# A decoder's first self attention: another order of the score units, maxima moved by DMA, results gathered by DMA

## The chip, the cores and the metric

The kernel runs on one core of one Trainium2 chip. The metric is the time of one execution on the device, in microseconds; several runs are timed and their median is given. A separate execution is profiled. In the profile, PE is the matrix engine, PEld its weight loads, DVE the vector engine, ACT the scalar engine, POOL the general engine, and SP an engine that here only issues DMAs. L191 means line 191 of the kernel before.

## What is computed

Two decoder layers in a row on x, a tensor of 4 x 1024 x 256 floats. Only the first step is changed, a causal self attention with 16 heads of 16, its output projection, the addition of x and a layer norm:

```python
q, k, v = jnp.split(x @ w_in.T + b_in, 3, axis=-1)      # to 16 heads of 16
scores = jnp.einsum('bhqd,bhkd->bhqk', q * 0.25, k)
scores = scores + causal_bias                           # 0 below the diagonal, -inf above
attn = jax.nn.softmax(scores, axis=-1)
out = jnp.einsum('bhqk,bhkd->bhqd', attn, v)
x = _layernorm(x + (out.reshape(4, 1024, 256) @ w_out.T + b_out))
```

The later steps (cross attention, feed forward, and the second layer) are the same in both kernels.

## The kernel before, in words

The function self_attention (L186) handles 16 groups of four heads: group s belongs to batch s//4. The heads' queries and keys lie spread over the 128 partitions, head g of the group in partitions 32g to 32g+15 (tiles qp and kp). A score matmul therefore contracts over a strip of 32 rows of PE, and a unit works on two heads: pair 0 means the strips of heads 0 and 1, pair 1 those of heads 2 and 3.

Scores are computed twice. An **a unit** (L312) computes scores with queries on the output partitions, and DVE takes maxima over keys from PSUM (L332, L348). There are 18 of them per group, nine of each pair. For the diagonal blocks (units 7 and 8) a matmul of the identity with a mask is added after the scores (L346, recorded at L191). When a group's maxima are complete, L356 joins and negates them; L366 turns them with eight transposes, and L370 adds them to the queries, into row 16 of each strip of a second tile, qs. The keys hold a one in that row, so a **b unit** (L380), which computes the scores again with keys on the output partitions, yields scores less the maximum. ACT takes their exponential (L399), POOL clears what is above the diagonal (L402), and weighted (L420, recorded at L191, output acc) multiplies with the values. A value tile has 17 columns per head, the last of which is one, so that the sum of the exponentials comes out as a 17th row. ACT copies acc to SBUF (L439), L451 transposes it, DVE divides (L454, L455), L467 transposes back, and out_projected (L472) applies the output weights and adds to x.

The order of the work is written out by hand. at(when, f, ...) records an event, and all events run in order of when; PE instructions, DMAs and some others keep that order on their engine. A slot of T = 20 steps belongs to one group's a units: place j (0 to 17) of slot s stands at 20s+1+j and issues, together and round by round, one a unit of group s and one b unit of the group before, two places behind (L542 to L551). What stands between two places, in the gap, runs on the full array: the projections of later queries and keys (L275, four matmuls of 512 columns as two events per slot), values (L258), transposes, and the weighted sums (L420), which are split into pieces so that some gaps take 384 columns and others 128 (L525 to L538). Seven PSUM banks rotate among scores, projections and transposes (pool ps_l0a), and one holds acc. Queries and keys are spread over the strips by DMAs on SP's queue (L293), four per tile, of 64 KB each.

The units' strips come from these lines:

```python
rows = [slice(64 * pair + 32 * g, 64 * pair + 32 * g + 32) for g in range(2)]
...
units.append((a_unit, s, (7, 8, 0, 1, 2, 3, 4, 5, 6)[j // 2], 1 - j % 2))
sb, jb = divmod(18 * (s - 1) + j - 2, 18)
if 0 <= sb < 4 * NB:
    units.append((b_unit, sb, jb // 2, jb % 2))
```

Of the kernel before, what the change touches and what calls it, by code (L numbers as in the profile page):

```python
# [16 lines left out]
P = 128  # L17
# [12 lines left out]
def decoder_kernel(ctx: ExitStack, tc: tile.TileContext, a: dict, out: bass.AP):  # L30
# [155 lines left out]
    def self_attention(wk, pss, psa):  # L186
# [29 lines left out]
        vts, nmps, nmts = [], [], []  # L216
        for i in range(2):
            vt = wk.tile([P, NC, 17 * H + 16], F32, tag=f"v{i}", name=f"v{i}", bufs=1)
            nc.gpsimd.memset(vt, 1.0)
            vts.append(vt)  # L220
            nmp = wk.tile([P, 4, NC, 3], F32, tag=f"nmp{i}", name=f"nmp{i}", bufs=1)
            nc.gpsimd.memset(nmp, -3.0e38)
            nmps.append(nmp)
            nmt = wk.tile([P, NC, 4, 32], F32, tag=f"nmt{i}", name=f"nmt{i}", bufs=1)
            nc.gpsimd.memset(nmt, 0.0)
            nmts.append(nmt)

        bo2 = wk.tile([P, E], F32, tag="bo2", name="bo2", bufs=1)
        t = bank()
        for e in range(2):  # L230
            mm(t[:, :E], l0a_bv[:, e : e + 1].to_broadcast([P, P]), l0a_wo[:, e, :], e == 0, e == 1)
        nc.vector.tensor_tensor(bo2, t[:, :E], l0a_bo, ALU.add)
# [6 lines left out]
        xTs, ons, sts, qss, pts, accs, ots = {}, {}, {}, {}, {}, {}, {}  # L239
# [18 lines left out]
        def values(b, i):  # L258
            t = bank()
            for j in range(2):  # L260
                c = 2 * i + j
                for e in range(2):
                    mm(
                        t[:, j * E : (j + 1) * E],
                        xTs[b][:, e, c * P : (c + 1) * P],
                        l0a_w[:, e, 2 * E :],
                        e == 0,
                        e == 1,
                    )
            (nc.vector.tensor_copy, nc.scalar.copy)[i % 2](  # L270
                vts[b % 2][:, 2 * i : 2 * i + 2, : 17 * H].rearrange("p c (h r) -> p c h r", r=17)[:, :, :, 0:16],
                t.rearrange("p (c h d) -> p c h d", c=2, h=H),
            )

        def projected(kind, i, q):  # L275
            w0, bias, scale = {"k": (E, l0a_bk, 1.0), "q": (0, bq4, 0.25)}[kind]
            b, h = divmod(i, 2)
            if q == 0:
                sts[kind, i] = wk.tile([P, S], F32, tag="s" + kind, name="s" + kind, bufs=1)
            t = bank()  # L280
            for e in range(2):
                mm(
                    t,
                    l0a_w[:, e, w0 + h * P : w0 + (h + 1) * P],
                    xTs[b][:, e, q * 512 : (q + 1) * 512],
                    e == 0,
                    e == 1,
                )
            nc.scalar.activation(
                sts[kind, i][:, q * 512 : (q + 1) * 512], t, AF.Identity, bias=bias[:, h : h + 1], scale=scale  # L290
            )

        def spread(kind, s):  # L293
            pads = {"k": kpads, "q": qpads}[kind]
            pad = pads[s % len(pads)]
            st = sts[kind, s // 2]
            for g in range(4):
                r = 64 * (s % 2) + 16 * g
                pe(nc.sync.dma_start(out=pad[32 * g : 32 * g + 16, :], in_=st[r : r + 16, :]))
# [12 lines left out]
        def a_unit(s, u, pair):  # L312

            t = [bank() for _ in range(2)]
# [20 lines left out]
            else:  # L335
                q0 = 4 * (u - 7)
                for j in range(4):
                    cols = slice((q0 + j) * P, (q0 + j + 1) * P)
                    rounds.append([
                        (t[g][:, j * P : (j + 1) * P], qt[rows[g], cols], kt[rows[g], cols], j == 0, False)  # L340
# [3 lines left out]
                def after():  # L344
                    for g in range(2):
                        mm(t[g], ident_bf, cmask4.rearrange("p j n -> p (j n)"), False, True)  # L346
# [8 lines left out]
        def highest(s):  # L355
            nc.vector.tensor_reduce(  # L356
                nmts[s % 2][:, :, :, 16], nmps[s % 2].rearrange("p g q i -> p q g i"), AX.X, ALU.max, negate=True
            )

        def shifted_queries(s):  # L360
            nmt = nmts[s % 2]
            qs = qss[s] = wk.tile([P, S], F32, tag="qs", name="qs")
            for q in range(2):
                t = bank()
                for j in range(4):
                    pe(nc.tensor.transpose(  # L366
                        t[:, j * P : (j + 1) * P], nmt[:, 4 * q + j, :, :].rearrange("p g r -> p (g r)"), ident
                    ))
                cols = slice(q * 512, (q + 1) * 512)
                nc.vector.tensor_tensor(qs[:, cols], t, qpads[s % 2][:, cols], ALU.add)  # L370
# [49 lines left out]
        def weighted(s, qh, i, pieces, first=False, last=False):  # L420
# [6 lines left out]
            for kc, c0, q0, n in pieces:  # L427
                for g in range(4):
                    mm(
                        acc[32 * g : 32 * g + 32, q0 : q0 + n],  # L430
                        vts[b % 2][:, kc, 17 * (4 * t4 + g) : 17 * (4 * t4 + g) + 32],
# [4 lines left out]
            if last:  # L436
                if qh == 0:
                    ots[s] = wk.tile([P, S], F32, tag="ot", name="ot")
                nc.scalar.copy(ots[s][:, qh * 512 : (qh + 1) * 512], acc)  # L439

        def normalised(s, i):
            b, t4 = divmod(s, 4)
            if t4 == 0 and i == 0:
                ons[b] = wk.tile([P, NC, E], F32, tag="on", name="on", bufs=1)
            ot = ots[s]
            c0 = 4 * i
            on = ons[b][:, :, t4 * 64 : (t4 + 1) * 64].rearrange("p c (g d) -> p c g d", g=4)
            t = bank()
            for j in range(4):
                c = c0 + j  # L450
                pe(nc.tensor.transpose(t[:, j * P : (j + 1) * P], ot[:, c * P : (c + 1) * P], ident))  # L451
            v = t.rearrange("p (c g r) -> p c g r", c=4, g=4)
            rs = small.tile([P, 4, 4], F32, tag="rs8", name="rs8", bufs=2)
            nc.vector.reciprocal(rs, v[:, :, :, 16])  # L454
            nc.vector.tensor_tensor(  # L455
                on[:, c0 : c0 + 4],
                v[:, :, :, 0:16],
                rs.unsqueeze(3).to_broadcast([P, 4, 4, 16]),
                ALU.mult,
            )  # L460

        def turned_back(b, e, q):
            if (e, q) == (0, 0):
                ots[b, "n"] = wk.tile([P, 2, S], F32, tag="onT", name="onT", bufs=1)
            t = bank()
            for j in range(4):
                pe(nc.tensor.transpose(  # L467
                    t[:, j * P : (j + 1) * P], ons[b][:, 4 * q + j, e * P : (e + 1) * P], ident
                ))
            nc.scalar.copy(ots[b, "n"][:, e, q * 512 : (q + 1) * 512], t)  # L470

        def out_projected(b, c):  # L472
            onT = ots[b, "n"]
            t = bank()[:, :E]
            for e in range(2):
                mm(t, onT[:, e, c * P : (c + 1) * P], l0a_wo[:, e, :], e == 0, e == 1)
            y = wk.tile([P, E], F32, tag="y0", name="y0")
# [10 lines left out]

        T = 20
        for b in range(NB):  # L490
            t0 = 4 * b * T
            for i in range(4):
                q, e = divmod(i, 2)
                if b:
                    at(t0 - 2 * T + (3.5, 7.5, 9.5, 11.5)[i], x_transposed, b, e, q)
                else:
                    at(-60 + i + q, x_transposed, b, e, q)
                at(t0 + (i // 2 - 1) * T + (3.5, 7.5)[i % 2], values, b, i)
                at(t0 + 5 * T + 3.5 + 4 * i, turned_back, b, e, q)
            for c in range(NC):  # L500
                u = (117.5, 135.5, 151.5, 155.5, 157.5, 171.5, 175.5, 177.5)[c]
                at(t0 + u if b < 3 else t0 + 6 * T + c, out_projected, b, c)
        for i in range(2 * NB):
            t0 = 2 * i * T
            for q in range(2):
                if i == 0:
                    at(-57.5 + 2 * q, projected, "k", i, q)
                    at(-57.4 + 2 * q, projected, "q", i, q)
                else:
                    at(t0 - 2 * T + ((13.5, 17.5) if i % 2 == 0 else (9.5, 13.5))[q], projected, "k", i, q)  # L510
                    at(t0 - T + (9.5, 13.5)[q], projected, "q", i, q)
            for j in range(2):
                at(t0 + (j - 1) * T + 2.6 if i else -50 + j, spread, "k", 2 * i + j)
                at(t0 - (1 - j) * T + (16.5, 2.7)[j] if i else -50 + j, spread, "q", 2 * i + j)
        for s in range(4 * NB):
            at((s + 1) * T + 0.3, highest, s)
            at((s + 1) * T + 1.4, shifted_queries, s)
            if s < 3:
                at(s * T + 0.7, later_x, s + 1)
            for i in range(2):  # L520
                at((s + 2) * T + 1.5 + 4 * i, normalised, s, i)
            t0 = (s + 1) * T

            full = {0: (3, 7, 9, 13), 1: (9, 13), 2: (13, 17), 3: (3, 7, 9, 13)}
            for i, place in ((0, 6), (4, 14), (5, 16), (7, 22)):  # L525
                qh, kc = (0, 0) if i == 0 else (1, i - 3)
                n = 512 if (place + 1) % T in full[(s + 1 + place // T) % 4] else 384
# [1132 lines left out]
```

## Time and profile before

| what | us |
|---|---|
| median of 3 runs | 2229.46 |
| lowest and highest | 2228.82, 2235.07 |
| the profiled execution's own time | 2231.37 |
| its span in the profile | 2229.6 |
| first and last maximum L356 (groups 0 and 15) | 63.95, 704.82 |
| first instruction of the next step on PE | 750.12 |
| slot 3, from L356 to L356 | 42.20 |
| PE, DVE, ACT, POOL busy in that slot | 42.20, 27.10, 22.57, 6.30 |
| DMA of 64 KB to qp or kp, from issue to landing | 2.3 |

The changed stage is the first third of the span. A busy time is the time in which at least one instruction of the engine runs; matmuls are pipelined, and the profile models their ends, so the duration of a matmul row is longer than its share. The distance between the start of one group of matmuls and the start of the next is the safer measure. A matmul on f32 is recorded as two instructions, which the text calls passes. In a row of the timeline the columns are start, duration, engine, line, operation, output and inputs, the rows and columns of the array, the shape and the number of instructions joined in the row.

### The profile page before, as it was taken

The numbers are of one execution on the slowest core, as the hardware profiler recorded it, in microseconds if no ns is written. First come the engines' busy times: TensorE is split into PE (matmuls) and PEld (weight loads), VectorE is DVE, ScalarE is ACT, GpSimd is POOL, SyncE is SP. The second block draws the span as 40 slices with busy tenths as digits, with TensorE's granted clock in tenths as the row PEclk, the third lists the DMA queues.
The fourth block names the chain that finished last, engine by engine and source line by source line (L and its number), as shares of the span: only waits on it lengthen the run. The fifth ranks groups of instructions, "written<-read, shape, count | busy, mean of one in ns | idle before, by whom it ended". The sixth has DMA issues, their size and how long they took to land.

```text
span 2229.6 us, 39020 instructions
## 1 busy us (share of the span) xinstructions
PE 2100.6 (94%) x14708; PEld 1255.9 (56%) x14708; DVE 1491.3 (67%) x3287; ACT 1119.0 (50%) x2861; POOL 510.4 (23%) x1113
## 2 busy tenths in 40 slices
PE   7999999999999899989899989989999999999996
PEld 4554554555454456556556556656666655565654
DVE  4766667776775556658997888886972465555644
ACT  1455554554555365556666655554543234545444
POOL 1111111111111265445455443000000111111102
PEclk9999999999999999999999999999999999999998
DMA  4101100000000100000000100000000010010101
GB/s 111 39 6 53 37 9 15 11 16 15 6 16 1 39 1 20 1 1 1 1 1 1 34 1 22 1 0 1 1 1 1 2 20 15 15 29 10 29 1 38
DMA packets 24445, 34.85 MB, mean 16 GB/s; under 512 B 5953, under 2 KB 19649, under 8 KB 24257
## 3 DMA queue, kind: packets, MB, share of 16 engines
q1 hardware_dynamic: 22640, 31.20, 6.1%
q8 instruction: 117, 1.92, 0.4%
q10 hardware_dynamic: 1616, 1.16, 0.2%
q14 instruction: 72, 0.58, 0.1%
HBM read 15.56 MB, written 4.19 MB: 9 GB/s over the span
## 4 chain that ended last, share of the span: by engine, by line
PE 71%; DVE 20%; ACT 6%; issue 1%; POOL 1%; DMA 1%; SPq 0%; ACTq 0%; POOLq 0%; DVEq 0%
PE s L191 21%; PE t L590 15%; PE s L1196 10%; PE s L590 8%; PE acc L191 6%; DVE gt L946 4%; PE acc L1196 3%; PE t L774 2%; ACT u L749 2%; DVE nmp L332 2%; DVE x L169 1%; DVE nmx L745 1%; DVE bnst L136 1%; DVE gt L956 1%; DVE ht L932 1%
## 5 line engine op out<-in xcount | busy, mean ns | idle before, releaser
L399 ACT ACTIVATE p<-s 128x512 f32<-128x512 f32 x576 | 312.2, 595 | 291.9 <-PE s L191 283.7
L332 DVE TENSOR_REDUCE nmp<-s 128x1 f32<-128x512 f32 (+3 forms) x640 | 298.6, 522 | 153.8 <-PE s L191 153.0
L191 PE MATMUL s<-qs,kp 32*128 32x512 f32 (+3 forms) x1536 | 347.9, 521 | 0.0
L191 PE MATMUL s<-kp,qp 32*128 32x128 f32 (+3 forms) x2304 | 327.7, 407 | 2.4 <-DMA qp<-sq 2.1
L757 POOL TENSOR_SCALAR p<-u,rs 128x128 f32<-128x128 f32 x512 | 215.9, 441 | 284.8 <-DVE rs L753 185.0
L191 PEld LDWEIGHTS s<-kp,qp 32*128 32x128 f32 x2304 | 165.5, 189 | 136.1 <-ACT p L399 46.2
L402 POOL TENSOR_SCALAR_AFFINE_SELECT p<-p 128x256 f32<-128x256 f32 x256 | 99.6, 407 | 567.8 <-ACT p L399 567.8
L749 ACT ACTIVATE u<-s,nmx 128x154 f32<-128x154 f32 x512 | 192.9, 393 | 46.7 <-DVE nmx L745 30.6
L154 POOL TENSOR_TENSOR rstd<-ve,neghalf 128x4 f32<-128x4 f32 (+1 forms) x56 | 58.6, 1046 | 573.6 <-DVE ve L152 569.2
L191 PE MATMUL acc<-p,v 128*32 128x384 f32 (+3 forms) x2016 | 167.9, 420 | 0.1
L191 PEld LDWEIGHTS s<-qs,kp 32*128 32x128 f32 x1536 | 138.8, 183 | 29.1 <-DVE nmp L332 8.4
L590 PE MATMUL t<-xT,xw 128*128 128x512 f32 x256 | 123.3, 605 | 11.8 <-DVE xT L677 8.4
L1353 DVE TENSOR_REDUCE nmt<-s 128x3 f32<-128x462 f32 (+1 forms) x192 | 99.0, 578 | 45.6 <-PE s L1196 45.6
L745 DVE TENSOR_REDUCE nmx<-s 128x4 f32<-128x616 f32 x128 | 100.9, 788 | 39.5 <-PE s L590 38.2
L590 PE MATMUL t<-v,pt 128*128 128x256 f32 x512 | 116.5, 380 | 8.2 <-DVE pt L1105 8.2
L590 PE MATMUL t<-xw,ot 128*128 128x256 f32 x512 | 119.0, 387 | 2.7 <-ACT qt L731 2.6
L946 DVE SCALAR_TENSOR_TENSOR gt<-ht,cw,gt 128x256 f32<-128x256 f32 x256 | 116.4, 500 | 6.5 <-ACT gt L942 5.3
L590 PEld LDWEIGHTS s<-kt,qt 64*128 64x128 f32 x1024 | 75.9, 186 | 72.2 <-issue 50.8
L590 PE MATMUL s<-qt,xT 128*128 128x512 f32 x256 | 115.1, 592 | 0.0
L590 PEld LDWEIGHTS t<-v,pt 128*128 128x128 f32 x512 | 95.8, 190 | 30.5 <-DVE pt L1105 9.8
L348 DVE TENSOR_REDUCE nmp<-s 128x4 f32<-128x512 f32 x128 | 82.4, 686 | 44.8 <-PE s L191 44.4
L749 ACT ACTIVATION_READ_ACCUMULATOR u<-s,nmx 128x1 f32 x512 | 106.4, 208 | 0.0
(259 smaller groups left out, 3851.0 us busy)
## 6 DMA issues: line engine op xcount, KB each, us to landing
qp<-sq SPq DMA_DIRECT2D x128, 64.0 KB, 2.3
kp<-sk SPq DMA_DIRECT2D x64, 64.0 KB, 2.3
out_dram<-x SPq DMA_DIRECT2D x8, 512.0 KB, 2.9
x<-in_x_dram SPq DMA_DIRECT2D x3, 1024.0 KB, 6.5
wf<-in_L_ffn_w_dram SPq DMA_DIRECT2D x2, 1024.0 KB, 6.0
xw<-in_L_xattn_wk_dram SPq DMA_DIRECT2D x1, 1024.0 KB, 6.5
xw<-in_L_xattn_wq_dram SPq DMA_DIRECT2D x1, 1024.0 KB, 5.0
xw<-in_L_xattn_wv_dram SPq DMA_DIRECT2D x1, 1024.0 KB, 5.0
```

What stands on the lines that cost most here:

```text
L191: pe(nc.tensor.matmul(o, l, r, start=start, stop=stop))
L332: nc.vector.tensor_reduce(nmp[:, 2 * pair + g, qc, i : i + 1], t[g][:, c0 : c0 + n], AX.X, ALU.max)
L348: nc.vector.tensor_reduce(nmp[:, 2 * pair + g, q0 : q0 + 4, 0], t[g].rearrange("p (j n) -> p j n", j=4), AX.X, ALU.max,)
L399: nc.scalar.activation(p[:, g, :], t[g], AF.Exp)
L402: nc.gpsimd.affine_select(out=v, in_=v, compare_op=ALU.is_ge, fill=0.0, base=0, pattern=[[0, 2], [1, P]], channel_multiplier=-1,)
L590: pe(nc.tensor.matmul(o, l, r, start=start, stop=stop))
L745: nc.vector.tensor_reduce(nmx.rearrange("p i g -> p g i"), t, AX.X, ALU.max, negate=True)
L749: nc.scalar.activation(u[:, 2 * i + g, :], t[:, g, i, :], AF.Exp, bias=nmx[:, i, g : g + 1], accum_out=ssum[:, i, g : g + 1],)
L757: nc.gpsimd.tensor_scalar(p[:, h * P : (h + 1) * P], u[:, h, :P], rs[:, h : h + 1], 1.0, ALU.mult, ALU.mult)
L946: nc.vector.scalar_tensor_tensor(g, ht[:, i, k : k + N], cw[:, hc, k : k + 1], g, ALU.mult, ALU.add)
L1196: pe(nc.tensor.matmul(o, l, r, start=start, stop=stop))
L1353: nc.vector.tensor_reduce(nmts[s % 2][:, 3 * u : 3 * u + n, g, 17], ts[g][:, : n * LK].rearrange("p (c k) -> p c k", k=LK), AX.X, ALU.max, ...
```

## The change

The change rewrites how the pieces of this step follow each other, and three of the paths between engines.

- **Order of the a units.** The diagonal units stand at places 1, 3, 5 and 7, and the others follow in the order 4, 5, 6, 0, 1, 2, 3, with both pairs of each (a_order). The b units stand four places behind instead of two (DELAY).
- **Mask first.** The mask matmul opens the accumulation in the gap ahead of a diagonal unit (causal_mask), which takes its two banks there.
- **Maxima.** The queries are copied to qs by one DMA (second_queries). The joined maxima, 32 columns, are turned by one transpose, copied by ACT to SBUF and written to row 16 of the strips by four DMAs (maxima_turned).
- **Results.** A head has 24 columns in the value tile, 16 values and 16 shared ones for two heads, so that a sum of exponentials comes out in 16 rows. Eight DMAs per group gather values and sums into tiles on and den, untransposed (gathered). DVE takes the reciprocal of den in pieces of 128x512, and POOL multiplies (divided). The output projection reads the product as it is.
- **Equal pieces.** Weighted sums are one event per pair of units, in the odd gaps, values and projections have pieces of 256 columns.
- The bias of the output projection is computed in a later gap, the first queries are spread by ACT's queue, and the last results are gathered in two halves, partly by ACT's queue.

```diff
-        def shifted_queries(s):
-            nmt = nmts[s % 2]
-            qs = qss[s] = wk.tile([P, S], F32, tag="qs", name="qs")
-            for q in range(2):
-                t = bank()
-                for j in range(4):
-                    pe(nc.tensor.transpose(
-                        t[:, j * P : (j + 1) * P], nmt[:, 4 * q + j, :, :].rearrange("p g r -> p (g r)"), ident
-                    ))
-                cols = slice(q * 512, (q + 1) * 512)
-                nc.vector.tensor_tensor(qs[:, cols], t, qpads[s % 2][:, cols], ALU.add)
+        def second_queries(s):
+            qs = qss[s] = wk.tile([P, S], F32, tag="qs", name="qs")
+            pe(nc.sync.dma_start(out=qs, in_=qpads[s % 2]))
+        def maxima_turned(s):
+            t = bank()[:32, :P]
+            pe(nc.tensor.transpose(t, hms[s].rearrange("p g c -> p (g c)"), ident))
+            rows = wk.tile([32, P], F32, tag="mrow", name="mrow")
+            nc.scalar.copy(rows, t)
+            for g in range(4):
+                pe(nc.sync.dma_start(
+                    out=qss[s][32 * g + 16 : 32 * g + 17, :].rearrange("p (c n) -> p c n", c=NC),
+                    in_=rows[NC * g : NC * g + NC, :],
+                ))
...
+        diagonal = {1: (7, 0), 3: (7, 1), 5: (8, 0), 7: (8, 1)}
+        others = iter([(u, pair) for u in (4, 5, 6, 0, 1, 2, 3) for pair in range(2)])
+        a_order = [diagonal[j] if j in diagonal else next(others) for j in range(18)]
+
+        def causal_mask(s, j):
+            t = masks[s, j] = [bank() for _ in range(2)]
+            for g in range(2):
+                mm(t[g], ident_bf, cmask4.rearrange("p j n -> p (j n)"), True, False)
+
+        def a_unit(s, j):
+            u, pair = a_order[j]
+            t = masks.pop((s, j)) if j in diagonal else [bank() for _ in range(2)]
...
-        def normalised(s, i):
...
-        def turned_back(b, e, q):
...
+        def gathered(s, c0=0, n=S, queue=None):
...
+            cols = slice(c0, c0 + n)
+            for g in range(4):
+                r = 64 * (t4 % 2) + 16 * g
+                up = 32 * g + 16 * (g % 2)
+                down = 32 * g + 16 * (1 - g % 2)
+                pe(nc.sync.dma_start(out=ons[b][r : r + 16, e, cols], in_=ots[s][up : up + 16, cols]))
+                pe((queue or nc.sync).dma_start(out=dens[b, e][r : r + 16, cols], in_=ots[s][down : down + 16, cols]))
+
+        def divided(b, e, q):
+            cols = slice(512 * q, 512 * q + 512)
+            den, on = dens[b, e][:, cols], ons[b][:, e, cols]
+            nc.vector.reciprocal(den, den)
+            nc.gpsimd.tensor_tensor(on, on, den, ALU.mult)
...
+        def gap(s, j):
+            return (s + j // 18) * T + 1.5 + j % 18
...
+                        at(gap(2 * i - (2 if kind == "k" else 1), 6 + 2 * q), projected, kind, i, q)
...
+            at((s + 1) * T + 0.3, highest, s)
+            at(gap(s + 1, 0) - 0.1, maxima_turned, s)
+            at(gap(s, 4.3), second_queries, s)
...
+            for i in range(9):
+                g = gap(s + 1, 2 * i + 3 + DELAY)
+                for qh, kc, c0 in b_sets[i]:
+                    if (i, qh) == (2, 1):
+                        continue
+                    n = width(qh, kc)
+                    last = (i, qh) == (2, 0) or (i, kc) == (8, 7)
+                    at(g, weighted, s, qh, i, [(kc, c0, 512 - n, n)], i in (0, 3), last)
...
+            if s < 4 * NB - 1:
+                at(gap(s + 2, 5.3), gathered, s)
+            else:
+                at(gap(s + 1, 11.2), gathered, s, 0, 512, nc.scalar)
+                at(gap(s + 2, 5.3), gathered, s, 512, 512, nc.scalar)
+            for j in diagonal:
+                at(gap(s, j - 1) + 0.3, causal_mask, s, j)
...
                 if s < 4 * NB:
-                    units.append((a_unit, s, (7, 8, 0, 1, 2, 3, 4, 5, 6)[j // 2], 1 - j % 2))
-
-                sb, jb = divmod(18 * (s - 1) + j - 2, 18)
+                    units.append((a_unit, s, j))
+
+                sb, jb = divmod(18 * (s - 1) + j - DELAY, 18)
                 if 0 <= sb < 4 * NB:
                     units.append((b_unit, sb, jb // 2, jb % 2))
```

The reciprocals of a batch (divided) stand in the gaps after places 8 and 10 of the slots 4b+3 and 4b+5; for the last batch, after place 5 of slots 15 and 17 and place 12 of slot 16 (in slot 15 the build has the two behind the reduces of place 9).

## The prediction

> **What bounds the kernel now.** I read the page's busy table first, then the chain that ended last, then the busy times of whole slots, then single places of the timeline. A slot is one pass of the loop over groups of four heads (18 places); it runs from one maximum L356 to the next.
>
> ```profile
> PE 2100.6 (94%) x14708; PEld 1255.9 (56%) x14708; DVE 1491.3 (67%) x3287; ACT 1119.0 (50%) x2861; POOL 510.4 (23%) x1113
> ...
> PE s L191 21%; PE t L590 15%; PE s L1196 10%; PE s L590 8%; PE acc L191 6%; DVE gt L946 4%; PE acc L1196 3%; PE t L774 2%; ACT u L749 2%; DVE nmp L332 2%; DVE x L169 1%; DVE nmx L745 1%; DVE bnst L136 1%; DVE gt L956 1%; DVE ht L932 1%
> ```
>
> TensorE leads, and the changed stage (L191) is the largest entry. Two slots of that stage, busy times by engine:
>
> ```profile
> 144.76:186.96 42.20, 42.20 (x414) 21.72 (x410) 27.10 (x57) 22.57 (x41) 6.30 (x17) 1.00 0.15 39
> 186.96:229.19 42.23, 42.23 (x414) 21.75 (x414) 27.11 (x56) 22.57 (x41) 6.22 (x16) 1.00 0.15 39
> ```
>
> PE is busy for all 42.2 us at a granted clock of 1.00; DVE needs 27.1 and ACT 22.6. So in this stage a microsecond of PE is a microsecond of time, and work taken from DVE is worth nothing by itself.
>
> Now one place, an a unit (scores for the maxima, kp,qp) and a b unit (scores for the exponentials, qs,kp) issued together:
>
> ```profile
> 165.29 0.70 PE L191 MATMUL s<-kp,qp 32*128 32x512 f32 x2
> ...
> 165.30 0.70 PE L191 MATMUL s<-qs,kp 32*128 32x512 f32 x2
> ...
> 165.82 0.59 PE L191 MATMUL s<-kp,qp 32*128 32x512 f32 x2
> 165.84 0.59 PE L191 MATMUL s<-qs,kp 32*128 32x512 f32 x2
> 166.36 0.30 PEld L191 LDWEIGHTS s<-xT,qkv 128*128 128x128 f32 x2 [0.76 <-DVE nmp L332]
> ```
>
> Each f32 matmul is recorded as two passes. Eight passes of 512 columns are over in 166.36-165.29 = 1.07 us. From the full-array matmuls (four passes of 512 from 166.36 to 168.27) one such pass takes about 0.43 us, so eight in a row would need 3.4: the four 32-row strips of the array work side by side, a on one pair of strips and b on the other. A b unit alone takes as long:
>
> ```profile
> 719.50 1.13 PE L191 MATMUL s<-qs,kp 32*128 32x512 f32 x4
> ...
> 720.56 1.13 PE L191 MATMUL s<-wo,onT 128*128 128x256 f32 x4
> ```
>
> That is 1.06 us, so the second unit is free **when it stands on the other two strips**. What it costs on the same strips is shown in the first slot, where a units stand alone, on alternating pairs:
>
> ```profile
> 44.23 1.99 PE L191 MATMUL s<-kp,qp 32*128 32x512 f32 x12
> 46.15 1.99 PE L191 MATMUL s<-qkv,xT 128*128 128x256 f32 x8
> 48.07 1.14 PE L191 MATMUL s<-kp,qp 32*128 32x512 f32 x8
> 49.15 1.12 PE L191 MATMUL s<-xT,qkv 128*128 128x512 f32 x2
> ```
>
> Two units on two pairs: 49.15-48.07 = 1.08. Three units, the third on the first one's pair: 46.15-44.23 = 1.92. A unit that shares strips costs 0.85 us more, two passes of 0.43.
>
> **Part 1: which strips the units take.** Before, L549 gives a the pair 1-j%2 and b (two places behind) the pair j%2: never the same. After, b still has j%2 (four places behind), but a_order gives a, for j = 0 to 17, the pairs 0,0,1,1,0,0,1,1, then 0,1,0,1,... Both are equal at j = 0, 3, 4, 7 and 8 to 17: 14 of 18 places. The tile positions in the built program say the same. Almost every gap holds full-array work (weighted in the odd ones, projections, values, output projections and masks in the even ones), which all four strips must finish first, so a neighbour can't fill the idle pair. Between one full-array matmul and the next I count 183 stretches with both units on one pair, and 13 of four units, spread evenly, where nothing stands between two places. The 183 cost 0.85 each: **+156 us**. DVE and ACT have room, so nothing hides it.
>
> **Part 2: PE work removed and added.** Gone: the 8 transposes of L366 per slot (1.09 us as one group), 8 of L451 (two groups of 0.58, from 156.74 to 157.32), 4 of L467 (0.58): 16 x 2.83 = -45. Added: one transpose per slot, 0.25 with its change of tile: +4. Projections in 64 pieces of 256 columns instead of 32 of 512: the columns are the same, and a group pays about 0.2 once (1.91 for four passes that need 1.71), so +6; values in 32 pieces instead of 16: +3. Weighted runs in 143 groups instead of 207 at about 0.14 (0.99 for 0.85 of columns): -9. The mask's two matmuls only move ahead of their place. Sum: **-41**.
>
> **Part 3: DVE.** It loses the two L370 (0.68 each) and two pairs L454/L455 (0.25+0.42) per slot: 2.7 us that lay beside PE, worth nothing in most slots. In the slots from 313.77, 360.88, 490.55, 537.67 and 662.77 the chain runs for 5 to 7 us through DVE (nmp, x); PE's own idle time from 63.95 to 704.82 is 640.87-633.37 = 7.5. With longer places these holds vanish: **-10** (0 to -20).
> New are 16 reciprocals of 128x512. No such row exists; the nearest:
>
> ```profile
> L753 DVE RECIPROCAL rs<-ssum 128x4 f32<-128x4 f32 x128 | 22.1, 173 | 49.6 <-ACT u L749 44.9 <-POOL p L757 2.7 <-issue 1.2
> L454 DVE RECIPROCAL rs<-s 128x16 f32<-128x16 f32 x32 | 7.9, 248 | 10.1 <-PE s L451 10.1
> ...
> L857 DVE RECIPROCAL sc<-am 128x8 f32<-128x8 f32 x4 | 0.8, 194 | 0.0
> ```
>
> From 4 to 8 elements it grows by 5.3 ns each, from 8 to 16 by 6.8; at the whole 248 ns per 16 it would be 15.5. That gives 2.8, 3.6 and 7.9 us; I take 3.6, the slope nearest in size. Queued behind each are the next place's reduces (1.3 to 1.4), and PE waits for their banks: the pool has seven, and a place takes four or five. A place with its gap lasts about 2.9, its reduces 1.4, so 1.5 of the 3.6 is cover, the banks in hand give about 1.5 more, and some 0.6 is left in twelve of them, 8 in all; in slot 15 two stand back to back, 7.2 less 3, so 4: **+12** (0 to +60 at 7.9).
> [...]
>
> **Part 4: DMAs, with their cover.** SP gets 13 more issues per slot (four maxima, one copy of the queries, eight gathers) at about 0.62 (2.49 for four): 8 us of a slot near 50. The copy of the queries (512 KB; such loads took 2.9 to 5.6) is issued a whole slot before use. The maxima: exponentials ahead on ACT 1.1, copy 0.4, four issues 2.5, landing 2.3 (the 64 KB row) = 6.3 us after place 0. The b unit that reads them stands at place 4, behind three places (1.07+1.07+1.92) and four gaps (4 or more): 8 us. Hidden; each microsecond missing would cost 15, one per slot. The gathers wait for the copy of the slot's last result and are due at the reciprocal three places later: 1.3+8x0.62+2.3 = 8.6 against 8 to 9, even, and any lateness is in the range of part 3. POOL's 16 products (the 128x512 row: 1.27) run where POOL is busy 6 of 42 us.
>
> **Part 5: both ends.** At the start the bias matmuls (2.04) move off the head and four query issues (2.44) go to ACT's queue beside SP's: **-4** (0 to -6). At the end b stands two places later, and the path from the last result to the projections is ACT copy 0.9, issues and landing 4.9, reciprocal 3.6, product 1.3 = 10.7, where transposes and evictions took 743.20-740.54 = 2.7; the same path stands once more ahead of the first four projections, but four projections fewer remain at the end. Sum **+12** (0 to +25).
>
> **Sum.** 156-41-10+12-4+12 = +125 on the profiled execution's 2231.4 (its span is 2229.6): 2356. That execution lies 2 above the median 2229.5, so **2354 us**.
>
> **Rivals.**
> 1. The shared strips cost nothing: the idle pair takes up the following work. Then the rest of the sum, -31, stands: 2198. For it: units in neighbouring places do run together where nothing is between them. Against it: full-array work is between nearly all, and 49.15 and 166.36 start only when all strips are done. It decides below (156-125)/183 = 0.17 us per clash. Chance 0.06.
> 2. A pass on a shared pair takes 0.53, the distance of the two passes in the place above (165.82-165.29), not 0.43: +0.21 x 183 = +38: 2392. Against it: the three units in 1.92. Chance 0.12.
> 3. DVE becomes the wait: reciprocals near 7.9 or gathers that land late hold PE 3 us each, 14 x 3 = 42 instead of 12: 2384. Chance 0.12.
> 4. Half the clash is hidden, since a's banks come free earlier and waits elsewhere shrink: 156/2: 2276. Chance 0.08.
>
> [...]
>
> My forecast has 0.62. The range **2285 to 2405** takes in rivals 2 and 3 and leaves out 1, most of 4, and both delays at once, under 0.2. About 0.3% (7 us) can be told from no change: faster 0.06, same 0.01, slower 0.93.
>
> **What would show it.** Right: a slot near 50 us with PE busy throughout; places of 1.9 us where kp,qp and qs,kp follow each other instead of starting together, at 14 of 18; no L366-like groups of eight. Wrong: places still at 1.07; PE idle behind a reciprocal or before the first qs matmul of a slot (parts 3, 4); reciprocals far from 3.6.

## The result and the profile after

| | us |
|---|---|
| changed kernel, median of 4 runs | 2359.8 (2353.08 to 2363.79) |
| kernel before in the same session, median of 4 | 2229.14 (2226.45 to 2235.07) |
| ratio, 95% interval | 1.058 [1.055, 1.061] |
| profiled execution, its span | 2363.79, 2361.3 |
| first and last maximum (now L362) | 62.21, 814.82 |
| first kt, the keys of the next step (DVE; L690 before, L691 now) | 888.7 (before 760.3) |

The change costs 131 us. The page of the changed kernel, busy times and the chain that ended last:

```profile
PE 2224.0 (94%) x14052; PEld 1306.6 (55%) x14052; DVE 1506.8 (64%) x3215; ACT 1115.9 (47%) x2901; POOL 528.7 (22%) x1127
...
PE s L191 28%; PE t L591 13%; PE s L1197 10%; PE s L591 7%; PE acc L191 6%; DVE gt L947 4%; PE acc L1197 3%; ACT u L750 2%; PE t L775 2%; DVE x L169 1%; DVE nmx L746 1%; DVE ht L933 1%; DVE gt L957 1%; DVE bnst L136 1%; PE t L1105 1%
```

PE has 656 instructions fewer and is busy 123 us longer, and the scores (s L191) grew from 21 to 28% of a longer chain. Two slots, one without and one with reciprocals (columns: stretch, its sum, busy PE, PEld, DVE, ACT, POOL, granted clock, DMA share, GB/s):

```profile
204.55:256.11 51.56, 51.56 (x389) 26.00 (x381) 25.30 (x52) 22.89 (x46) 6.22 (x16) 1.00 0.21 52
256.11:306.79 50.68, 50.68 (x383) 25.27 (x377) 33.38 (x61) 23.18 (x46) 8.71 (x18) 1.00 0.22 53
```

A slot grew from 42.2 to 51, PE is busy throughout at a granted clock of 1.00, and eight more us of DVE in the second slot don't lengthen it. A place in the first of them:

```profile
235.96 1.13 PE L191 MATMUL s<-kp,qp 32*128 32x512 f32 x4
236.92 1.02 PE L191 MATMUL s<-qs,kp 32*128 32x512 f32 x4
237.87 0.64 PE L191 MATMUL acc<-p,v 128*32 128x256 f32 x8
```

The b unit starts 0.96 after the a unit and not beside it. The place lasts 237.87-235.96 = 1.91, where 1.07 stood before.

To see where the 131 went, I gave each stretch of PE's timeline, from the start of one group of matmuls to the start of the next, to the kind of the first group. Waits are thus part of the group before them. Between the first and the last maximum:

| kind, us | before | after | no_shared_strips | no_shared_no_reciprocal |
|---|---|---|---|---|
| score places | 324.9 | 476.0 | 370.5 | 343.6 |
| weighted sums | 141.1 | 133.6 | 138.2 | 131.6 |
| projections, values | 72.3 | 78.5 | 84.0 | 80.1 |
| transposes | 43.7 | 7.3 | 7.5 | 7.5 |
| masks | 36.3 | 32.9 | 32.9 | 32.9 |
| output projections | 22.3 | 24.0 | 24.3 | 24.3 |
| all | 640.9 | 752.6 | 657.8 | 620.3 |

After against before: +111.7, of it places +151.1 and all the rest -39.4. The stretch from the last maximum to the next step grew from 55.5 to 73.9, +18.4. The start gave -1.7 and the later steps +3.4. (The columns of the two other kernels are used below.)

### The profile page after: what moved, and what is told of

Same layout as the page of the kernel before. It is cut to its first block, busy times and chain, and to the rows that moved or that the text cites. A ratio compares the mean times of both kernels' runs of the same rounds, so it can differ in the third digit from the quotient of the medians.

```text
span 2361.3 us, 38057 instructions
## 1 busy us (share of the span) xinstructions
PE 2224.0 (94%) x14052; PEld 1306.6 (55%) x14052; DVE 1506.8 (64%) x3215; ACT 1115.9 (47%) x2901; POOL 528.7 (22%) x1127
## 4 chain that ended last, share of the span: by engine, by line
PE 72%; DVE 18%; ACT 6%; issue 1%; DMA 1%; POOL 1%; SPq 0%; ACTq 0%; POOLq 0%; DVEq 0%
PE s L191 28%; PE t L591 13%; PE s L1197 10%; PE s L591 7%; PE acc L191 6%; DVE gt L947 4%; PE acc L1197 3%; ACT u L750 2%; PE t L775 2%; DVE x L169 1%; DVE nmx L746 1%; DVE ht L933 1%; DVE gt L957 1%; DVE bnst L136 1%; PE t L1105 1%
## 5 line engine op out<-in xcount | busy, mean ns | idle before, releaser
L191 PE MATMUL s<-kp,qp 32*128 32x128 f32 (+3 forms) x2304 | 343.5, 414 | 3.4 <-DMA qp<-sq 3.4
L191 PE MATMUL s<-qs,kp 32*128 32x512 f32 (+3 forms) x1536 | 322.2, 504 | 2.4 <-DVE nmp L339 1.6
L191 PEld LDWEIGHTS s<-kp,qp 32*128 32x128 f32 x2304 | 177.9, 191 | 163.8 <-issue 62.5
L191 PEld LDWEIGHTS s<-qs,kp 32*128 32x128 f32 x1536 | 139.6, 189 | 89.2 <-issue 51.2
L191 PE MATMUL acc<-p,v 128*32 128x512 f32 (+3 forms) x1536 | 159.4, 505 | 1.9 <-ACT ot L443 1.8
```

The lines of the kernel that those rows point to most:

```text
L191: pe(nc.tensor.matmul(o, l, r, start=start, stop=stop))
```

## The experiments

All times are medians; a ratio is to the kernel before in the same session. Its median lay between 2229 and 2235 in these sessions, so a difference between sessions is taken from the ratios, times 2232.

| kernel | us | ratio, interval |
|---|---|---|
| all_shared_before | 2428.3 | 1.088 [1.086, 1.091] |
| b_on_the_other_pair | 2298.9 | 1.030 [1.028, 1.032] |
| no_shared_strips | 2267.3 | 1.015 [1.013, 1.017] |
| no_shared_late_projection | 2252.2 | 1.009 [1.007, 1.011] |
| after_no_reciprocal | 2341.8 | 1.048 [1.046, 1.050] |
| no_shared_no_reciprocal | 2226.3 | 0.996 [0.995, 0.998] |
| no_shared_late_split2 | 2225.5 | 0.996 [0.994, 0.998] |
| no_shared_late_recip_later | 2253.2 | 1.009 [1.006, 1.011] |
| no_shared_late_split2_banks | 2222.7 | 0.997 [0.995, 0.998] |
| after_banks | 2357.4 | 1.057 [1.055, 1.058] |
| after_late_split2 | 2334.0 | 1.046 [1.044, 1.048] |
| half_exponentials | 2211.1 | 0.992 [0.990, 0.993] |

The theory was that of the prediction: shared strips make the loss, and what remains is a small gain. The rival was that DVE's reciprocals and the gathers make a large part of it.

**Shared strips put into the kernel before.**

```diff
-                    units.append((a_unit, s, (7, 8, 0, 1, 2, 3, 4, 5, 6)[j // 2], 1 - j % 2))
+                    units.append((a_unit, s, (7, 8, 0, 1, 2, 3, 4, 5, 6)[j // 2], j % 2))
```

> The kernel before, with one edit: the a unit at place j takes the pair j%2, which is the pair of the b unit beside it. Between full-array matmuls the built program then has 256 stretches with both units on one pair of strips, against none. Theory (a unit that shares strips costs 0.85 us of PE and nothing hides it): +256 x 0.85 = +218, so about 2447 us, and places of 1.92 us instead of 1.07. Rival (the shared strips are not what costs, the neighbouring work fills the idle pair): within 1% of 2229. Rival (half is hidden, because the banks come free earlier): about 2338.

Measured 2428.3, +196 for 256 stretches: 0.77 each, a little under the 0.85 of the theory. Nothing but the pair of the a unit differs, so shared strips alone can cost more than the whole change.

**Fewer of them in the changed kernel**, by the b unit's pair:

```diff
-                    units.append((b_unit, sb, jb // 2, jb % 2))
+                    units.append((b_unit, sb, jb // 2, 1 - jb % 2))
```

> The changed kernel, with one edit: the b unit takes the pair 1-jb%2. Shared places go from 14 to 4 of 18, shared stretches from 183 to 56 in the built program. Theory: -127 x 0.85 = -108, so about 2252 us. Rival (the added time comes from the reciprocals, the DMAs and their waits): 2360 within 1%.

**And none**, by the order of the a units:

```diff
-        diagonal = {1: (7, 0), 3: (7, 1), 5: (8, 0), 7: (8, 1)}
-        others = iter([(u, pair) for u in (4, 5, 6, 0, 1, 2, 3) for pair in range(2)])
+        diagonal = {1: (7, 0), 2: (7, 1), 5: (8, 0), 6: (8, 1)}
+        others = iter([(u, pair) for u in (4, 5, 6, 0, 1, 2, 3) for pair in (1, 0)])
```

> The changed kernel, with two edits in a_order: the diagonal units at places 1, 2, 5 and 6 and the pairs of the others in the order 1, 0, so that a has the pair 1-j%2 everywhere and no place is shared. The masks of two diagonal units move to odd gaps. Theory: -183 x 0.85 = -156, so about 2204 us, below the kernel before, the rest of the change being worth -30 and its longer end costing some 16. Since the places are short again, the reciprocals have less cover: up to 20 more, 2224. Rival (DMAs and reciprocals carry the added time): 2300 or more.

Measured 2298.9 and 2267.3. The strips are the largest cause, but by the ratios removing them gives 62 for 127 stretches and 95 for all 183, some 0.5 each and not 0.85, and the kernel without them is still 34 us slower than before, where 8 to 28 faster was expected. Something else holds once the places are short. Slots with and without reciprocals, in no_shared_strips:

```profile
140.24:186.74 46.50, 44.83 (x377) 20.71 (x377) 30.72 (x53) 22.86 (x44) 8.74 (x18) 0.96 0.24 58
186.74:228.94 42.20, 42.20 (x385) 21.83 (x389) 25.27 (x53) 22.72 (x45) 6.21 (x16) 1.00 0.27 64
```

The slot that holds two reciprocals is 4.3 longer; PE has gaps there, and its granted clock is 0.96. The timeline of that slot shows how:

```profile
167.38 3.34 DVE L464 RECIPROCAL den<-den 128x512 f32<-128x512 f32 x1
...
170.63 2.41 DVE L339 TENSOR_REDUCE nmp<-s 128x1 f32<-128x512 f32 x4
...
171.32 1.12 PE L191 MATMUL s<-qs,kp 32*128 32x512 f32 x2 [1.05 <-DVE nmp L339]
...
173.82 1.22 PE L191 MATMUL s<-kp,qp 32*128 32x512 f32 x2
```

The reduces of two places queue behind the reciprocal, PE waits 1.05 for a bank, and the place at 173.82 then runs at half speed (1.22 for rows of 0.70). The granted clock in stretches of 1 us (the third column from the end):

```profile
172.00:173.00 1.00, 1.00 (x5) 0.58 (x4) 1.00 (x2) 0.53 (x1) 0.05 (x1) 0.98 0.00 0
173.00:174.00 1.00, 1.00 (x7) 0.35 (x8) 0.05 (x1) 0.14 (x2) 0.00 (x0) 0.50 0.07 16
...
175.00:176.00 1.00, 1.00 (x12) 0.16 (x8) 0.07 (x1) 0.00 (x0) 0.00 (x0) 0.50 0.39 57
176.00:177.00 1.00, 1.00 (x12) 0.18 (x12) 1.00 (x2) 0.91 (x2) 0.00 (x0) 0.81 0.67 111
```

The hold is time in which PE stands, and about 3.4 us at 0.50 come after it. That the hold brings the second part isn't shown: the slot below has the same wait of 1.05 (at 531.73), and its clock stays at 1.00.

```profile
499.89:545.51 45.62, 44.27 (x373) 21.67 (x373) 37.15 (x74) 22.34 (x43) 9.71 (x19) 1.00 0.17 36
```

It is 3.3 longer than the same slot without reciprocals (42.28), the other slots with reciprocals, the last left aside, 5.0 to 5.8. So by estimate, from these differences, the clock is some 2 us of what such a slot loses, and the standing the larger part.

**The last batch's first four output projections, later.**

```diff
-                places[:4] = [(s0 + 4, j) for j in (14, 15, 16, 17)]
+                places[:4] = [(s0 + 5, 14), (s0 + 5, 16), (s0 + 6, 4), (s0 + 6, 14)]
```

> As no_shared_strips, and the first four output projections of the last batch stand two slots later, beside the last four, so that PE does not wait for the product of the first half of the last results. In the changed kernel PE waits 7.0 us there and then has a granted clock of 0.57 for some 16 us. Theory (that wait and the lower clock behind it are on the path): 8 to 15 us below no_shared_strips. Rival (the end is set by the chain of the last DMAs, the reciprocal and the projections, and the four more projections there take the time back): within 3 us of it.

Measured 2252.2, -15. In the changed kernel this is the end of its stage, on PE's rows:

```profile
843.08 1.22 PE L191 MATMUL s<-wo,on 128*128 128x256 f32 x2 [6.64 <-POOL on L465]
844.23 2.08 PE L191 MATMUL s<-qs,kp 32*128 32x512 f32 x4
```

and in stretches of 2 us:

```profile
844.00:846.00 2.00, 2.00 (x5) 0.51 (x4) 1.56 (x4) 0.00 (x0) 0.00 (x0) 0.50 0.00 0
...
856.00:858.00 2.00, 2.00 (x6) 1.18 (x4) 0.21 (x2) 1.09 (x2) 0.00 (x0) 0.50 0.03 8
858.00:860.00 2.00, 2.00 (x13) 0.51 (x16) 1.66 (x4) 0.00 (x0) 0.00 (x0) 0.78 0.00 0
```

A projection stands in PE's order ahead of the last b units and waits 6.64 for the product of the gathered results. Then PE runs at 0.50 for some 15 us, although it is busy; a b unit alone takes 2.0 and not 1.06. Moved behind the b units, the projection finds its product ready, and from the last maximum to the next step it is 55.1, as before the change.

**Reciprocals left out**, with the strips of the changed kernel and without shared ones:

```diff
-            nc.vector.reciprocal(den, den)
```

> The changed kernel with the reciprocals left out: the results are multiplied by the sums and not divided (so the output differs from the reference). 16 instructions of 3.34 us fall from DVE. My theory, that the reciprocals of the slots lie beside a PE which the shared strips keep busy (PE busy 749.9 of the 752.6 us between the first and the last maximum) and that only those at the end are exposed: about 7 in the slots and 7 at the end, so about 2346. Rival, that the reciprocals' holds are a large part of the loss whatever the strips do: 40 or more, 2320 or below.

> No stretch with two units on one pair of strips, and the reciprocals left out as in the run beside it (the output differs from the reference). In no_shared_strips the slots with reciprocals last 45.0 to 48.0 us and the others 40.3 to 43.6, about 4.5 more in each of 8 slots. My theory, that the reciprocals show once the places are short: 8 x 4.5 = 36 and 7 at the end less, about 2224. Rival, that the longer slots have another cause (the late gathers' issues, the output projections): as little as in the changed kernel, 2267 - 14 = 2253.

They take 22 us in the changed kernel (11.3 of it between the maxima, 752.6 against 741.3) and 42 in the one without shared strips (37.5 between the maxima). The theory had 14 and 43, the rivals 40 or more and 14, so the theory holds, with its first number too small. Of the 11.3 only 2.5 lie in the six slots with reciprocals before the last; 8.7 lie in the last slot (50.55 against 41.82), where the granted clock was 0.83 on average. There the changed kernel has

```profile
783.80:793.52 9.72, 9.72 (x51) 5.87 (x47) 3.75 (x10) 2.42 (x5) 1.53 (x4) 0.50 0.17 29
...
793.52 6.57 DVE L464 RECIPROCAL den<-den 128x512 f32<-128x512 f32 x2
```

The clock fell ahead of this slot's reciprocals, so that all of this part is theirs isn't shown; it fell once more behind them, from 800.9 to 804.3. With short reciprocals (after_late_split2) it was 1.00 on average over all slots. Seen from the other side: shared strips cost 95 with reciprocals and 116 without. The two causes cover each other, so their prices don't add.

**The same reciprocals in short pieces, and later ones.** The first edit spreads eight pieces of 128 columns over eight gaps, kept in order among the reduces (the lines that fix DVE's order are left out here); the second was to move the whole ones by three places:

```diff
-            cols = slice(512 * q, 512 * q + 512)
+            cols = slice(128 * q, 128 * q + 128)
...
-                for q in range(2):
+                for q in range(8):
...
+                        at(gap(s0 + 2 * e + 3, 8.2 + q), divided, b, e, q)
```

```diff
-                    at(gap(s0 + 4, 12.2) if last else gap(s0 + 2 * e + 3, 8.2 + 2 * q if b < NB - 1 else 5.5), divided, b, e, q)
+                    at(gap(s0 + 4, 12.2) if last else gap(s0 + 2 * e + 3, 11.2 + 2 * q if b < NB - 1 else 5.5), divided, b, e, q)
```

> no_shared_late_projection (2252.2), with reciprocal and product in eight pieces of 128 columns, one to a gap from place 8 on, kept in the written order among DVE's reduces. The same DVE work in short pieces. If a reciprocal holds PE by its length (3.34 us ahead of the next reduces), the 4.5 us of eight slots go and 36 us less remain, about 2216, under the kernel before. If what holds is the lateness of the gathers that the first piece waits for, nothing or a few us: 2245 to 2252.

> no_shared_late_projection (2252.2), with the whole reciprocals three places later (gaps after places 11 and 13 instead of 8 and 10), when the gathers have long landed. If lateness of the gathers (0.8 us of wait in front of the reciprocals seen) is a main part of the hold: 15 or more less, 2237 or below. If the length of the reciprocal holds: 7 less at most, 2245 to 2252.

Measured 2225.5 (-29) and 2253.2 (no change). The second number says nothing, since the reciprocals didn't move. Their order on DVE isn't fixed in that kernel, and the build left them where they were: in every slot the order of reduces and reciprocals is that of no_shared_late_projection. The first reciprocal of slot 3 in no_shared_late_projection, no_shared_late_recip_later and no_shared_late_split2:

```profile
164.20 3.35 DVE L464 RECIPROCAL den<-den 128x512 f32<-128x512 f32 x1 [0.82 <-DMA on<-ot]
...
160.01 3.35 DVE L464 RECIPROCAL den<-den 128x512 f32<-128x512 f32 x1 [0.55 <-issue]
...
158.93 0.95 DVE L464 RECIPROCAL den<-den 128x128 f32<-128x128 f32 x1 [0.49 <-issue]
```

That is 21.4, 21.1 and 21.1 us after the maximum that opens the slot. What speaks against the lateness of the gathers is the first edit alone: its first piece starts as early or late as the whole reciprocal, DVE stands before it much as before, and yet the 4 to 5 us are gone. So what holds PE is 3.34 us of DVE in one go. (The whole reciprocals stood in the written order too, so fixing the order changed nothing for them.) The same slots in no_shared_late_split2, with the same DVE work:

```profile
137.88:178.98 41.10, 41.01 (x377) 19.79 (x373) 30.87 (x59) 22.61 (x44) 9.91 (x24) 1.00 0.27 66
178.98:221.18 42.20, 42.20 (x385) 21.84 (x388) 25.26 (x53) 22.73 (x45) 6.25 (x16) 1.00 0.25 64
```

DVE is as busy as in no_shared_strips (30.87 and 30.72), PE's gaps are gone and the clock is 1.00. This kernel still has every part of the change, three of them rearranged, and takes 0.4% less than the one before.

**Both of these edits with the strips of the changed kernel.** The edits are those of no_shared_late_split2 without the order of the a units.

> The changed kernel with its strips as they are, and with the two other edits of no_shared_late_split2 (the last batch's first four output projections later, reciprocals in eight pieces). Without shared strips these two took 42 us (2267.3 to 2225.5). Theory, that the shared strips hide most of the reciprocals: leaving them out took 18 to 22 here, the late projections 15 at the end, in part the same wait, so 20 to 35 less: 2325 to 2340. Rival, that the three edits add up whatever the strips do: 42 less, 2318 or below.

Measured 2334.0, 27 less by the ratios, where the same edits took 43 without shared strips: again the strips hide part of it.

**Where the transposes' gain is.** Even without shared strips and reciprocals the places stand at 343.6 against 324.9 before, half of the 36 that the transposes gave. In no_shared_late_split2 a place after a weighted gap mostly lasts 1.07, one after a projection 1.3 to 1.6:

```profile
208.75 0.68 DVE L339 TENSOR_REDUCE nmp<-s 128x1 f32<-128x512 f32 x1
208.78 0.59 ACT L402 ACTIVATE p<-s 128x512 f32<-128x512 f32 x1
209.11 0.70 PE L191 MATMUL s<-kp,qp 32*128 32x512 f32 x2
...
209.12 1.05 PE L191 MATMUL s<-qs,kp 32*128 32x512 f32 x2
```

The b unit's first row should end after 0.70, like the a unit's; it takes 1.05, since its second head starts 0.35 late. At 209.47 it does, just after the last reduce (209.43) and the last exponential (209.37) of the place before. A projection takes one of the seven banks, and with four for each place the place behind it needs two that the place before still holds. In the kernel before a projection took a bank too, yet all 38 places behind projections or values last 1.1 there. Such a gap took 1.8 to 1.9 with the larger pieces and takes 1.1 now, so the banks had longer to come free; this is read from the two traces, and larger pieces were not put back. The first try at this:

```diff
+            if len(units) == 2 and units[0][2] not in diagonal:
+                t = [bank() for _ in range(4)]
+                units = [(*unit, t[i::2]) for i, unit in enumerate(units)]
```

> no_shared_late_split2 (2225.5) with one more edit: the four banks of a place are given out a, b, a, b instead of a, a, b, b (not at the diagonal units, whose banks the mask takes). In that kernel's trace a place after a weighted gap mostly lasts 1.07 us, but 76 of the 85 after a gap with a projection, values or output projection last 1.3 (21), 1.4 (39) or 1.6 (16): such a gap takes a bank of its own, so the second head of the b unit gets the bank of the place before's second reduce, which ends 0.3 us too late. Theory, that this is where the transposes' gain went: 21 x 0.2 + 39 x 0.35 + 16 x 0.5 = 26 us less, about 2200. Rival, that the wait only moves to another bank (the exponentials' on ACT) or that the places are long for another reason: 2218 to 2228.

> The changed kernel (2359.8) with that edit of the banks alone. With shared strips 63 places after such gaps last 1.9 like the others, which is later than the bank comes free. Theory, that the shared strips hide the banks' wait: within 5 us of the changed kernel. Rival, that the banks hold in it too: 15 or more less.

Both stayed as they were. This is no evidence on the wait: every matmul waits for the same counts in the built program as without the edit, so the banks are not given out in the order of asking, and the edit only changed names. The second try makes the exponentials shorter (the p tiles are then six fixed ones, filled with ones at the start):

```diff
-                    nc.scalar.activation(p[:, g, :], t[g], AF.Exp)
+                    nc.scalar.activation(p[:, g, :256], t[g][:, :256], AF.Exp)
```

> no_shared_late_split2 (2225.5) with each exponential taken of the first 256 columns only (the other columns of the p tiles hold ones from the start, so the output differs from the reference; the matmuls are all there). The edit of the banks' names did nothing: the banks are not given out in the order of asking, and the waits of the built program stayed the same. In them the second head of a b unit waits for an ACT count, and in the trace its first pass starts 0.11 us after the second exponential of the place before (210.78, then 210.89). With 256 columns the two exponentials end about 0.35 us earlier, just before the pass is due. Theory, that this wait is what makes 76 places 1.3 to 1.6 instead of 1.07: up to 26 us less, about 2200, and those places near 1.07. Rival, that the reduces of DVE, which end within 0.1 us of the exponentials, hold the banks as well: the places stay and the time is 2217 to 2226.

Measured 2211.1, 10 less by the ratios. Of the 85 places after such gaps 38 now last 1.1 (4 before the edit), 38 still 1.4 and 9 longer. One of 1.4:

```profile
208.95 1.29 DVE L342 TENSOR_REDUCE nmp<-s 128x1 f32<-128x512 f32 x2 [0.70 <-PE s L191]
209.10 0.66 ACT L405 ACTIVATE p<-s 128x256 f32<-128x256 f32 x2 [0.54 <-PE s L191]
209.92 0.70 PE L191 MATMUL s<-kp,qp 32*128 32x512 f32 x2
209.94 1.05 PE L191 MATMUL s<-qs,kp 32*128 32x512 f32 x2
```

The exponentials end at 209.76, too early to matter; the b unit's second head starts at 209.94+0.35 = 210.29, just after the reduces (210.24). So both theory and rival hold in part: where the bank was held by an exponential the wait is shown, by its going; where it is held by a reduce it was seen in the timeline only. Shorter reduces were not tried.

## Why the prediction was right, and what in it was luck

The time, 2359.8 for 2354, and the forecast's mechanism hold: places of 1.91, slots near 50 us, PE busy 749.9 of 752.6. Step by step:

- **Part 1, +156.** As an account of what PE does it is right: the places grew by 151. As the price of the shared strips it is wrong: they cost 95 in this kernel. The step that doesn't hold is "DVE and ACT have room, so nothing hides it". Nothing hides it, but it hides other waits, which come back when it goes.
- **Part 2, -41.** Between the maxima -39.4: transposes -36.4, the smaller pieces of projections and values +6.2, weighted sums -7.5, masks and output projections -1.7. But a smaller piece takes a bank as a whole one does, and gives the place before less time to free its own. This was not in the sum; the shared strips hide it here. Without them the places are 18.7 longer than before (324.9 to 343.6, in which the pairs of places with nothing between also changed); the short exponentials took 13 off the places (353.7 to 340.9 in no_shared_late_split2), so the wait for banks is shown for a part.
- **Part 3, -10 and +12.** PE's idle time between the maxima fell from 7.5 to 2.7, -5. A reciprocal takes 3.34, for the 3.6 from the slope of the short rows. Fourteen of the sixteen lie between the maxima, and they cost 11.3 there. That it is so near to 12 is luck: twelve of them cost 2.5, where the prediction has 8 (its own 0.6 for each gives 7), and the last slot 8.7, where it has 4, most of it, by estimate, by the low clock (0.50 from 783.8 to 797.4 and from 800.9 to 804.3), which the prediction doesn't speak of. The reason given for the twelve, cover by long places, holds, but the long places are the shared strips themselves; without them the cost is 37.5, more than three times as much.
- **Part 4, hidden.** Right. Between the first and the last maximum PE waits for the joined maxima only once, 1.55 at the first, and no reciprocal of the slots waits long for a gather. The reciprocals in the changed kernel, over all sixteen:

```profile
L464 DVE RECIPROCAL den<-den x16: 3296/3340/3353, 178.1 to 871.4; 128x512 f32<-128x512 f32 x16
its engine sat idle before it (us, times) until:
  DMA den<-ot: 31.6, 2
```

  The two that waited for a DMA are not in the slots but at the end.
- **Part 5, -4 and +12.** The start gave -1.7. The end cost 18.4, inside its range: the path was seen, but not that a projection stands ahead of the b units in PE's order and that the clock is 0.50 behind the wait. Without shared strips the late projections undo it.
- **Rivals.** Rival 1 gave 2198 for strips that cost nothing; the kernel without shared strips takes 2267. It carries the other terms, -31, over to short places, for which they were not worked out: there all the rest of the change is worth +34. So the terms add up in the changed kernel, but none of them is a price by itself. Rival 4 (waits elsewhere shrink) described the coupling; its half was near, since 95 of 156 is 0.6, but the other costs, which it left alone, grew by as much. Rival 3 (DVE holds PE) is true of the kernel without shared strips, and of this one only by the 11.3 above, at most.
- **The reciprocal and the weight loads.** A reciprocal of 128x512 took 3.34 and one of 128x128 0.94, so 6.2 ns a column between the two. The b unit's weight loads add no time that is seen: a shared place takes 1.91, as the matmul passes alone give (1.06 and two of 0.43). In the place at 235.96 the b unit's loads (236.49 to 236.68) run beside the a unit's second passes (236.49 to 236.92), on the same strips.

## What to carry to other kernels

Before units are reordered, write down which strips of the array each pair of neighbours takes: here two units on one pair of strips ran one after the other, 1.91 for 1.07. A term that lengthens the bound engine can also hide the waits of the others (here the reciprocals cost 11.3 between the maxima with shared strips and 37.5 without), so a sum of terms can be right while each term's price by itself is not; take one away and look what surfaces. A long instruction on an engine that frees PSUM banks is better cut into pieces between the short ones: here 3.34 us in one go held PE, and the same work in pieces of 0.94 did not. And see in the trace that what an edit moves has moved, before its time is read.

## What the runs showed of the hardware

A lower clock followed some short holds of PE and not others. In no_shared_strips the longest idle stretch ahead of the fall to 0.50 at 173.0 was 1.05 us, with 1.6 us idle in all in the 8 us before it; the half clock lasted about 3.4 us. What makes it fall isn't shown: the same hold of 1.05 at 531.73 was followed by no fall, and in the changed kernel it fell at 783.8 with a single idle stretch of 0.61 in the 8 us before it, and stayed at 0.50 for 13.6 us. (Rows of score units can contain a wait of their second head, as above, so PE may stand more than its idle stretches say.) At the end of the changed kernel's stage the clock fell at 838.4, within a hold of 6.64, and some 15 us at 0.50 followed the hold, with PE busy in all of them. How long the lower clock lasts isn't shown either: after PE was at work again 3.4, 13.6 and some 15 us in these three cases.
